# One adaLN transformer block: batch 1's projections made in two halves of tokens, the second half beside batch 1's own attention

## The chip, the core and the metric

The kernel runs on one core of a Trainium2 chip. The core has five engines that each work through their own list of instructions in order: PE (TensorE, matrix products), DVE (VectorE), ACT (ScalarE), POOL (GpSimd) and SP (SyncE, which here issues nearly all DMA transfers). They wait for one another through semaphores. The metric is the time of one execution on the device, in microseconds (us). All data are float32.

## The reference

Two batches of 1024 tokens, width 1024, go through one block. `c` gives six modulation vectors per batch (`sa, ca, ga, sb, cb, gb`). Then:

```
h   = layernorm(x) * (1 + ca) + sa
qkv = clip(h @ Wqkv.T, -8, 8);  q, k = layernorm(q), layernorm(k)   (over all 1024 columns)
p   = softmax(q k^T / sqrt(32) + slope_h * (key - query), causal)   32 heads of 32
x   = x + ga * ((p v) @ Wout.T)
h   = layernorm(x) * (1 + cb) + sb
x   = x + gb * ((silu(h Wg ag) * (h Wu au)) @ Wd ad)                2752 wide
```

The causal mask is what matters for the change: the first 512 queries of a batch need the keys and values of the first 512 tokens only.

## The kernel before, in words

**Dense products.** `seven` makes a 256-token by 1024-column product as seven block products of a Strassen-Winograd scheme (`SEVEN`), each of four matmuls of 128x128 by 128x512 on PE, into two alternating banks of PSUM. It takes seven weight tiles of 1 MB each (`B11 B21 T2 T1 T3 B22 T4`, made or loaded by `weights_b`). The pool of these tiles holds one set, so a tile of the next set can be loaded only when the last product that uses its predecessor is done. `read` takes each product out of PSUM on ACT or DVE. In this text "a product" is one of the seven.

**Projections.** `projections(b, ...)` (L927) makes Q, K and V of batch `b`: for each `part` (0, 1, 2) it gets the weights and then runs over the four pairs `j` of token tiles, 256 tokens each. The operand `a` of a pair is loaded from DRAM (1.8 MB). For Q and K the rows are normalized (`normalize`) and, during the following products, transposed on PE and taken to DRAM (`turned`, `todo`). V goes to DRAM directly. When V of an odd pair is out, `ready.add((b, j // 2))` says that this half of the batch's tokens can be attended to. `side` is called after every product and takes one step of `down_weights`, the preparation of weights for the last stage (POOL subtractions and small DMAs).

**Attention.** `attention` (L1013) is a generator over batches, blocks of 512 queries (`qb`) and groups of four heads (`k`, eight of them). A group consists of units (`jb`): four of them in the first query block, eight in the second, each a block of 128 keys. A unit is: scores on PE (four matmuls with 32 rows, in two halves), exponentials on ACT (L1069), the causal mask on POOL for diagonal blocks (L1073), and, two units later (`LAG`), the weighted sum of values on PE (`weigh`) and a running sum of the exponentials on DVE and POOL (L1101). After a group, `settle` sums over keys on PE in the one bank that transposes use too. The scores of a unit need the PSUM of the unit before, which its exponentials release. `chunk` loads a group's queries, keys and values, two groups ahead; it waits for `ready`.

**What sets the order.** `together(att, dense, share)` walks the attention generator and, after each step, takes dense work until its planned amount `d` reaches `share(a)`, a function of the planned attention `a` so far. `share` (L1569) gives `LEAD + DENSE0` units of dense work to batch 0's attention and `DENSE1` to batch 1's; these three constants stand at L1359. If `chunk` finds its tokens not ready it yields None, and `together` takes a dense step at once, share or not. The dense work is `dense_work` (L1535): the last V pairs of batch 0, all of batch 1's projections, then the output projection (`output`) of batch 0 and of the first half of batch 1. Within this stage PE's order is kept as emitted; the other engines' lists, SP's too, are ordered by the framework's scheduler. After the attention the rest of the output projection and the feed-forward layer follow.

Of the kernel before, what the change touches and what calls it, by code (L numbers as in the profile page):

```python
# [480 lines left out]
def kernel(  # L481
# [20 lines left out]
    B, S, D = x.shape  # L502
    INTER = wg_t.shape[1]
    KC = D // P
    NT = S // P
# [27 lines left out]
    wt_dram = [  # L533
        dram.tile([P, 4, KC // 2, HALF], FP, tag=f"wt_{r}", name=f"wt_{r}") for r in range(4)
    ]
# [253 lines left out]
    def weights_b(pool, w, nm, sums, other=None, swap=False):  # L789

        made = other is None
        order = ("B11", "B21", "T2", "T1", "T3", "B22", "T4") if made else ("B11", "B21", "B12", "B22", "T1", "T2", "T3", "T4")
        bt = {
            q: (other if q == "B12" or q == "B22" and swap else pool).tile(
                [P, KC // 2, HALF], FP, tag=f"w{q}", name=f"w{q}_{nm}"
            )
            for q in order
        }  # L800
        for q in order:
            if q in BLOCKS:
                kh, n = BLOCKS[q]
                nc.sync.dma_start(
                    bt[q], w[ds(kh * D // 2, D // 2), ds(n * HALF, HALF)].rearrange("(k p) f -> p k f", p=P)
                )
            elif made:
                nc.sync.dma_start(bt[q], sums[:, PARTS[q]])
        if not made:
            for k in range(KC // 2):  # L810
                nc.vector.tensor_sub(bt["T1"][:, k], bt["B12"][:, k], bt["B11"][:, k])
                nc.vector.tensor_sub(bt["T2"][:, k], bt["B22"][:, k], bt["T1"][:, k])
            for k in range(KC // 2):
                nc.gpsimd.tensor_sub(bt["T3"][:, k], bt["B22"][:, k], bt["B12"][:, k])
            for k in range(KC // 2):
                nc.gpsimd.tensor_sub(bt["T4"][:, k], bt["B21"][:, k], bt["T2"][:, k])
            for q in ("T1", "T2", "T3", "T4"):
                nc.sync.dma_start(sums[:, PARTS[q]], bt[q])
        return bt

    def seven(a, bt, banks, read, between, grain):

        x, y = banks.pair()
        for c_, qa, qb_, q in SEVEN:
            bank = x if c_ == "x" else y
            first = q in ("P1", "P2", "P5")
            for j in range(KC // 2):
                matmul(
                    bank, a(qa, j), bt[qb_][:, j, :],
                    start=(first and j == 0), stop=(j == KC // 2 - 1), skip_group_check=True,  # L830
                )
                if j % grain == grain - 1 and j < KC // 2 - 1:
                    banks.made += 1
                    yield grain * MM
                    yield from between(q)
            read(q, bank)
            banks.made += 1
            yield grain * MM
            yield from between(q)
# [17 lines left out]
    def column(t, r):  # L857
        return lambda k: t[:, r + k : r + k + 1]
# [43 lines left out]
    def tokens(b, j, todo, ap_, xp, sm):  # L902

        a = ap_.tile([P, 7, KC // 2, P], FP, tag="a", name=f"a_{b}_0_{j}")
        xs = []
        for m in range(2):
            xt = xp.tile([P, D], FP, tag="xt", name=f"xt_{b}_{j}_{m}", bufs=2)
            nc.scalar.dma_start(xt, x[b, ts(2 * j + m, P), :])
            xs.append(xt)
        normalize(xs, xs, sm, f"x{b}_{j}")()  # L910
        for m in range(2):
            for g in range(2):
                def go(bank, m=m, g=g):
                    q = (("A11", "A12"), ("S3", "A22"))[m][g]
                    turned(
                        xs[m], bank, lambda k: a[:, SLOT[q], k % 4, :],
                        lambda k: modt[:, 1, k, b : b + 1], lambda k: modt[:, 0, k, b : b + 1], g,
                    )
                    if (m, g) == (1, 1):
                        sums_a(a, nc.vector, nc.gpsimd)  # L920
                        nc.sync.dma_start(hop_dram[b][j], a)
                todo.add(go)
        return a
# [3 lines left out]
    def projections(b, pools, banks, places, extra=None, other=None, side=lambda n, e: None):  # L927

        ap_, wp_, rawp, partp, qsp, xp, sm = pools
        todo = Todo(banks)
        made = {}
        if b == 0:
            made[0] = tokens(b, 0, todo, ap_, xp, sm)
        for part in range(3):
            bt = weights_b(wp_, wqkv_t[:, ts(part, D)], f"{b}_{part}", wt_dram[part], other, b == 0 and part == 1)
            for j in range(NT // 2):
                if b == 0 and part == 2 and j == NT // 4:
                    yield "mark"  # L940
                if b == 0 and part == 0:
                    if j == 0:
                        yield from todo.run(len(todo.list), True)
                    a = made.pop(j)
                    if j + 1 < NT // 2:
                        made[j + 1] = tokens(b, j + 1, todo, ap_, xp, sm)
                else:
                    a = ap_.tile([P, 7, KC // 2, P], FP, tag="a", name=f"a_{b}_{part}_{j}")
                    nc.sync.dma_start(a, hop_dram[b][j])
                if extra is not None:  # L950
                    extra(todo, part * (NT // 2) + j)
                raws = [
                    rawp.tile([P, D], FP, tag="raw", name=f"raw_{b}_{part}_{j}_{m}") for m in range(2)
                ]
                part_t = {}
                q0, n = (2 - b, places) if b or part or j else (5, 4)

                def read(q, bank):
                    if q in ("P1", "U2", "P5"):
                        part_t[q] = partp.tile([P, 512], FP, tag=q, name=f"{q}_{b}_{part}_{j}")  # L960
                        nc.scalar.copy(part_t[q], bank)  # L961
                        return
                    m, n = QUAD[q]
                    dst = raws[m][:, ts(n, HALF)]
                    if q == "U6":
                        nc.vector.tensor_scalar(dst, bank, CLIP, -CLIP, ALU.min, ALU.max)
                    else:
                        nc.vector.tensor_add(dst, part_t[MATE[q]], bank)  # L968
                        nc.vector.tensor_scalar(dst, dst, CLIP, -CLIP, ALU.min, ALU.max)

                yield from seven(
                    lambda q, i: a[:, SLOT[q], i, :], bt, banks, read, 
                    todo.places(q0, n, lambda e: side(part * (NT // 2) + j, e)), KC // 2
                )
                yield from todo.run(len(todo.list), True)
                if part == 2:
                    for m in range(2):
                        nc.sync.dma_start(v_dram[b][:, 2 * j + m, :], raws[m])
                    if j % 2:
                        ready.add((b, j // 2))  # L980
                    continue
                todo.first(normalize(raws, raws, sm, f"qk{b}_{part}_{j}"), b == 0)
                qs = qsp.tile([P, KC, 2, P], FP, tag="qs", name=f"qs_{b}_{part}_{j}")
                r_w, r_b = ((R_QW, R_QB), (R_KW, R_KB))[part]
                for m in range(2):
                    for g in range(2):
                        def go(bank, m=m, g=g, raws=raws, qs=qs, r_w=r_w, r_b=r_b, part=part, j=j):
                            turned(
                                raws[m], bank, lambda k: qs[:, k, m, :], column(vt, r_w), column(vt, r_b), g, b == 0
                            )  # L990
                            if (m, g) == (1, 1):
                                nc.sync.dma_start(
                                    qk_dram[b][part][:, :, ds(2 * j * P, 2 * P)],
                                    qs.rearrange("p k m t -> p k (m t)"),
                                )
                        todo.add(go)
# [359 lines left out]


    OUT_US = 112.0
    LEAD, DENSE0, DENSE1 = 16.0, 370.0, 136.0  # L1359

    def halves(half, jb):
        return (nc.vector, nc.gpsimd)[half]
# [213 lines left out]
    opools, _, bt, todo, _ = out_args  # L1576
# [99 lines left out]
    with ExitStack() as ff:  # L1676
# [9 lines left out]
        with ExitStack() as gu:  # L1686
# [62 lines left out]
            count = [0]  # L1749
# [22 lines left out]
            for s in range(NSB):  # L1772
# [66 lines left out]
                for n_, (oa, ob, frm, to) in enumerate(STAGES):  # L1839
# [11 lines left out]
                    part = {"g": {}, "u": {}}  # L1851
# [6 lines left out]
                    for e, (c_, qa, qb_, q) in enumerate(CHAIN):  # L1858
                        bt = bts[e] if e < len(bts) else moving(s, n_, e)
# [231 lines left out]
```

## Time and profile before

| | |
|---|---|
| median of 3 runs | 2853.81 us (2849.35 to 2857.14) |
| the profiled execution, its own time | 2848.94 us |
| its span | 2846.9 us |
| PE, DVE, POOL, ACT busy over the span | 95%, 51%, 46%, 24% |
| granted TensorE clock, mean | 0.984 |
| DMA | 579.14 MB, mean 203 GB/s |

The span falls into three parts. Up to 362 us: modulation vectors and batch 0's projections. From 362 to about 1331 us: attention of both batches, with dense work between its steps. From there to the end: the rest of the output projection and the feed-forward layer, which are nearly all PE.

Within the middle part, the first matmul of scores of each block gives four stages. Batch 0's first query block runs from 362 to 538 us, its second to 937 us; batch 1's first query block to 1061 us, its second to the end of the attention.

A line of a group of instructions gives the line of the kernel, engine, operation, tiles, shapes and count, then busy time, the mean of one in ns, and the idle time of the engine before them with what ended it. A line of the timeline gives start and duration in us, the instruction, and in brackets the idle time before it. PE executes one float32 matmul of the program as two instructions, so "x8" is a product of four matmuls.

### The profile page before, as it was taken

How to read it: one execution, taken by the hardware profiler on the slowest of the kernel's cores; microseconds unless marked ns; L12 is line 12 of the kernel's file. 1: busy time of each engine (PE TensorE's matmuls, PEld its weight loads, DVE VectorE, ACT ScalarE, POOL GpSimd, SP SyncE). 2: the span in 40 equal slices, each digit the busy share in tenths (PEclk: the TensorE clock that was granted, in tenths of full speed). 3: DMA queues.
4: the chain of work that ended last, by engine and by line, in shares of the span. 5: the costliest groups of instructions: out<-in, count | busy, mean ns of one | idle time of the engine just before them, and what ended most of it. 6: DMA issues, size and time to landing. Idle time of an engine off the chain costs nothing. (4 is left out here: it accounts for less than half of the span.)

```text
span 2846.9 us, 29933 instructions
## 1 busy us (share of the span) xinstructions
PE 2691.8 (95%) x10271; PEld 1328.0 (47%) x10271; DVE 1462.4 (51%) x2285; ACT 687.8 (24%) x1524; POOL 1296.2 (46%) x1270
## 2 busy tenths in 40 slices
PE   6999999999999888889999999999999998999998
PEld 2444433333333222223664444444444447888776
DVE  5766525566634457666644453544536355443442
ACT  1322243444344556554111010110101101000000
POOL 3312124545565665655447474455636431322352
PEclk9999999999999899999999999999999999999999
DMA  9877863766755554433687576675857668554552
GB/s 346 310 273 300 298 233 118 234 217 209 231 152 198 149 175 136 147 128 112 199 294 244 170 251 214 186 279 162 278 176 234 199 198 267 150 148 136 167 144 79
DMA packets 377573, 579.14 MB, mean 203 GB/s; under 512 B 21590, under 2 KB 278712, under 8 KB 366276
## 3 DMA queue, kind: packets, MB, share of 16 engines
q1 hardware_dynamic: 363928, 556.12, 59.9%
q10 hardware_dynamic: 13484, 21.02, 2.3%
q8 instruction: 84, 1.38, 0.2%
q14 instruction: 77, 0.63, 0.1%
HBM read 411.89 MB, written 165.17 MB: 203 GB/s over the span
## 5 line engine op out<-in xcount | busy, mean ns | idle before, releaser
L1069 ACT ACTIVATE p<-sc,kw 128x128 f32<-128x128 f32 (+3 forms) x1024 | 422.5, 515 | 356.9 <-PE sc L743 344.4
L743 PE MATMUL bank<-wT,a 128*128 128x512 f32 x768 | 356.8, 608 | 15.1 <-ACT P L961 8.5
L1101 POOL TENSOR_TENSOR p<-p,p 128x1024 f32<-128x1024 f32 (+3 forms) x128 | 262.5, 2051 | 174.0 <-PE av L743 142.0
L1101 DVE TENSOR_TENSOR p<-p,p 128x1024 f32<-128x1024 f32 (+3 forms) x192 | 250.2, 1314 | 143.2 <-POOL p L1073 85.2
L743 PE MATMUL bank<-wB,a 128*128 128x512 f32 x576 | 262.3, 601 | 1.4 <-DVE raw L968 0.9
L743 PE MATMUL sc<-cq,ck 32*128 32x512 f32 (+3 forms) x1536 | 192.7, 540 | 55.9 <-ACT p L1069 55.6
L743 PEld LDWEIGHTS bank<-wT,a 128*128 128x128 f32 x768 | 141.2, 193 | 190.7 <-issue 163.2
L1073 POOL TENSOR_SCALAR_AFFINE_SELECT p<-p 128x256 f32<-128x256 f32 x256 | 136.7, 548 | 195.6 <-ACT p L1069 192.2
L743 PE MATMUL av<-p,cv 128*32 128x512 f32 (+3 forms) x1536 | 170.7, 512 | 3.2 <-POOL p L1073 3.2
L743 PEld LDWEIGHTS bank<-wB,a 128*128 128x128 f32 x576 | 104.6, 190 | 144.3 <-issue 126.1
L743 PEld LDWEIGHTS sc<-cq,ck 32*128 32x128 f32 x1536 | 64.6, 186 | 193.6 <-ACT p L1069 108.0
L1863 PE MATMUL gy<-bt,sig 128*128 128x512 f32 x280 | 132.2, 594 | 7.0 <-DVE gX L1670 6.9
L1863 PE MATMUL uy<-bt,siu 128*128 128x512 f32 x280 | 131.6, 592 | 0.0
L1863 PE MATMUL gx<-bt,sig 128*128 128x512 f32 x280 | 131.6, 592 | 0.0
L1863 PE MATMUL ux<-bt,siu 128*128 128x512 f32 x280 | 131.6, 592 | 0.0
L743 PEld LDWEIGHTS av<-p,cv 128*32 128x32 f32 x1536 | 33.7, 109 | 122.5 <-issue 83.5
L1863 PEld LDWEIGHTS gy<-bt,sig 128*128 128x128 f32 x280 | 52.7, 190 | 76.1 <-issue 64.1
L1863 PEld LDWEIGHTS ux<-bt,siu 128*128 128x128 f32 x280 | 53.2, 190 | 67.0 <-issue 66.5
L1863 PEld LDWEIGHTS uy<-bt,siu 128*128 128x128 f32 x280 | 53.2, 190 | 67.0 <-issue 65.3
L1863 PEld LDWEIGHTS gx<-bt,sig 128*128 128x128 f32 x280 | 53.2, 190 | 67.0 <-issue 65.7
L1863 PE MATMUL ux<-bt,wuS 128*128 128x512 f32 x160 | 75.2, 592 | 0.0
L1863 PE MATMUL gx<-bt,wgS 128*128 128x512 f32 x160 | 75.2, 592 | 0.0
(415 smaller groups left out, 4459.8 us busy)
## 6 DMA issues: line engine op xcount, KB each, us to landing
bt<-bop_T SPq DMA_DIRECT2D x140, 512.0 KB
bt<-bop_B SPq DMA_DIRECT2D x99, 512.0 KB
a<-hop SPq DMA_DIRECT2D x20, 1792.0 KB
wm<-in_L_wmod_dram SPq DMA_DIRECT2D x48, 512.0 KB
wB<-in_L_attn_Wqkv_dram SPq DMA_DIRECT2D x21, 1024.0 KB
aq_S<-act_S SPq DMA_DIRECT2D x16, 1280.0 KB
qk<-qs SPq DMA_DIRECT2D x16, 1024.0 KB
act_S<-asS SPq DMA_DIRECT2D x30, 512.0 KB
```

The costliest lines, as they stand in the source:

```text
L743: return in_order(nc.tensor.matmul(*args, **kw_))
L1069: last_exp[0] = nc.scalar.activation(p[:, g, lo:hi], sp[:, g, lo:hi], AF.Exp, bias=kw[:, d, h_ : h_ + 1])
L1073: last_mask[0] = nc.gpsimd.affine_select(out=p[:, :, 0:P], in_=p[:, :, 0:P], pattern=[[0, 2], [1, P]], compare_op=ALU.is_ge, fill=0.0, bas ...
L1101: adders[b](half, jb).tensor_add(dst, dst, ps[half][:, :, 0:n])
L1863: nc.tensor.matmul(ps.rearrange("p (j t) -> p j t", j=NJ), ins[mat][qa][:, c2, :], bt[:, :, c2, :], start=(q in ("P1", "P2", "P5") and c2 ...
```

## The change

For batch 0 nothing changes in `projections` but names. For batch 1 the loop over the three parts is run twice, first with the pairs 0 and 1 (tokens 0 to 511), then with the pairs 2 and 3: Q, K, V of the first half, then Q, K, V of the second. Each of the six runs gets its weights by `weights_b`, so that the three sets of seven tiles are loaded twice. The first half becomes `ready` when its V is out. `n_pair`, a count of pairs made, replaces the computed number in the call of `side`. `DENSE0` goes from 370 to 280, and `DENSE1` from 136 to 226.

```diff
-        for part in range(3):
-            bt = weights_b(wp_, wqkv_t[:, ts(part, D)], f"{b}_{part}", wt_dram[part], other, b == 0 and part == 1)
-            for j in range(NT // 2):
+
+        halves_ = [range(NT // 2)] if b == 0 else [range(NT // 4), range(NT // 4, NT // 2)]
+        count = itertools.count()
+        for js, part in itertools.product(halves_, range(3)):
+            bt = weights_b(
+                wp_, wqkv_t[:, ts(part, D)], f"{b}_{part}_{js[0]}", wt_dram[part], other, b == 0 and part == 1
+            )
+            for j in js:
+                n_pair = next(count)
...
-                    todo.places(q0, n, lambda e: side(part * (NT // 2) + j, e)), KC // 2
+                    todo.places(q0, n, lambda e: side(n_pair, e)), KC // 2
...
-    LEAD, DENSE0, DENSE1 = 16.0, 370.0, 136.0
+    LEAD, DENSE0, DENSE1 = 16.0, 280.0, 226.0
```

## The prediction

> **What bounds the kernel now.** I read the page first: busy shares, then the 40 slices.
>
> ```profile
> PE 2691.8 (95%) x10271; PEld 1328.0 (47%) x10271; DVE 1462.4 (51%) x2285; ACT 687.8 (24%) x1524; POOL 1296.2 (46%) x1270
> ...
> PE   6999999999999888889999999999999998999998
> PEclk9999999999999899999999999999999999999999
> ```
>
> PE is the bound over the whole; only slices 13 to 18, batch 1's attention, show eights. The busy time of the four stages (start:end, total, then PE, PEld, DVE, ACT, POOL busy, granted clock, DMA share, GB/s):
>
> ```profile
> 362.00:538.00 176.00, 171.44 (x837) 65.00 (x836) 77.82 (x129) 73.54 (x184) 73.02 (x100) 0.99 0.51 171
> 538.00:937.00 399.00, 382.12 (x1724) 139.77 (x1728) 218.48 (x307) 171.96 (x401) 221.74 (x197) 0.98 0.65 214
> 937.00:1061.00 124.00, 105.84 (x668) 35.08 (x660) 59.22 (x94) 67.96 (x173) 80.52 (x98) 0.89 0.51 150
> 1061.00:1328.00 267.00, 230.06 (x1325) 73.04 (x1324) 175.47 (x244) 159.32 (x375) 161.08 (x129) 0.97 0.40 124
> ```
>
> PE idles 21 us of 575 beside batch 0 and 55 us of 391 beside batch 1, where no other engine is full either. So batch 1 is bound by a chain. PE's waits from 362 to 1328 us name it (total, times, longest):
>
> ```profile
> PE sc L743 <- ACT p L1069: 55.6, 55, 3.8
> PE bank L746 <- DVE raw L727: 8.0, 3, 5.2
> PE bank L743 <- DVE h2t L849: 4.5, 1, 4.5
> PE bank L743 <- issue: 4.0, 1, 4.0
> ```
>
> Scores wait for the exponentials of the unit before, which hold their PSUM. The timeline shows both regimes. Batch 0, one unit with a whole product:
>
> ```profile
> 863.73 1.14 PE L743 MATMUL sc<-cq,ck 32*128 32x512 f32 x8
> 864.80 1.06 PE L743 MATMUL av<-p,cv 128*32 128x512 f32 x8
> 865.80 3.70 PE L743 MATMUL bank<-wB,a 128*128 128x512 f32 x8
> 869.43 1.14 PE L743 MATMUL sc<-cq,ck 32*128 32x512 f32 x8
> ```
>
> Batch 1, one unit with half a product, one with none:
>
> ```profile
> 1154.25 1.14 PE L743 MATMUL sc<-cq,ck 32*128 32x512 f32 x8
> 1155.32 1.06 PE L743 MATMUL bank<-p,ones 128*32 128x512 f32 x8
> 1156.20 1.04 PE L743 MATMUL av<-p,cv 128*32 128x512 f32 x8
> 1157.18 1.98 PE L743 MATMUL bank<-wT_o,aoS 128*128 128x512 f32 x4
> 1159.09 1.14 PE L743 MATMUL sc<-cq,ck 32*128 32x512 f32 x8
> 1160.16 1.07 PE L743 MATMUL av<-p,cv 128*32 128x512 f32 x8
> 1162.77 1.14 PE L743 MATMUL sc<-cq,ck 32*128 32x512 f32 x8 [1.55 <-ACT p L1069]
> ```
>
> From scores to scores a unit takes the longer of PE's own work and the exponentials' turn. The first unit takes 5.7 us (all PE), the last 3.7 us with 2.1 us of PE work.
>
> Lastly the handover to the output projection, whose weights overlay the projections' buffers:
>
> ```profile
> 899.04 1.14 PE L743 MATMUL sc<-cq,ck 32*128 32x512 f32 x8
> 900.12 1.06 PE L743 MATMUL bank<-p,ones 128*32 128x512 f32 x8
> 905.16 3.75 PE L743 MATMUL bank<-wB_o,aoA 128*128 128x512 f32 x4 [3.98 <-issue]
> ...
> 899.14 0.38 SPq L804 DMA_DIRECT2D wB_o<-in_L_attn_Wout_dram x1
> ```
>
> The load goes out when V's last product ends; its first matmul starts 6.0 us later. PE idles 3.98 us, and the half product then takes 3.75 us instead of 1.98.
>
> **What the Trainium skill says.** "TensorE: Matmul & The Clock Gate", section "What's actually happening": an idle window of about 3.4 us puts PE's clock to half until it has been busy as long. The trace agrees: 3.75 against 1.98 us above, and a granted clock of 0.89 in the stage with most idle time. "GPSIMD Engine Reference", section 1: POOL's SBUF interfaces are shared with DVE when DVE reads two SBUF inputs. POOL's 1024-wide additions average 2051 ns over all forms, the full ones 2850 ns beside batch 1. "DMA: Bandwidth & Descriptors", section "Anatomy of one DMA": engines do not wait on semaphores, the issuing sequencer does; so a weight load that waits for PE holds back whatever stands behind it on SP. The trace shows such waits, 28 us in all from 400 to 900 us on the weight lines L804 and L808, with no PE wait put down to a load except the handover.
>
> **The change, part by part.**
>
> *What it removes.* No matmul. PE's order of both programs, laid against the trace of before instruction by instruction, gives whole products per stage: 31, 67, 9.5, 24 before and 24, 50, 19.5, 37.5 after. So 24 products leave batch 0's stages. Half a product and one turn of four transposes more are left after the last scores: 0.5 x 3.63 + 0.6, about 2 us.
>
> *What moving them is worth.* For each of the 192 units I took PE's work (3.63 us a product; a full block's scores 1.06 and values 1.06, narrower ones 0.85, 0.64, 0.43; settling 1.06; four transposes 0.67) and the shortest time such a unit shows in the trace: full block 3.7, the 384, 256 and 128 wide ones 3.0, 2.4, 1.8, a group's first 2.5; longer for the first group, whose exponentials are cut in 16 (5.5, 5.0, 3.2, 1.8), and a little for the second (4.3, 3.7, 2.5). The longer of the two, summed:
>
> | stage | measured | by the rule before (PE work) | left over | by the rule after (PE work) |
> |---|---|---|---|---|
> | batch 0, first block | 175.9 | 176.5 (172.0) | -0.6 | 150.7 (143.9) |
> | batch 0, second | 398.6 | 388.2 (383.4) | 10.4 | 338.6 (319.0) |
> | batch 1, first | 124.5 | 112.1 (93.3) | 12.4 | 148.7 (132.3) |
> | batch 1, second (no last unit) | 266.5 | 246.7 (217.4) | 19.8 | 285.1 (269.1) |
> | sum | 965.5 | 923.5 (866.1) | 42.0 | 923.1 (864.3) |
>
> The gain is nil: batch 1's losses to exponentials fall from 48 to 32 us, but batch 0's rise from 9 to 27. Products of 3.63 us are lumpy: with five in eight units instead of seven, some units have none. Units whose PE work is over 0.3 us short of their exponentials number 5, 4, 13, 26 before and 8, 16, 12, 12 after: 48 both times.
>
> *What is left over.* Before: the handover 6.4; one turn of K that waits for its normalization (7.9, at 738 us); one settling that waits for the shared bank (6.8, at 1078 us); two smaller in the last stage (2.5, 3.7); the rest about 1.1 per group. After, by stage: 0, 2, 14, 24. The second stage loses its handover and is less crowded. The third gets the handover, and keeps about 5.5 of 12.4 since denser work keeps PE's clock up. The last has 37.5 products for 24, so its 13 us of waits on DVE become about 17, plus 7 as before. Sum 40.
>
> *The handover moved.* In the built order its four last products of V stand in one run (14.5 us, because keys and values of the second half are not ready), and the output's first matmul directly behind them. The 2.1 us that lay between before are gone: 6.0 us idle plus 2.5 us at half clock, 8.5. Both are in the 14. Behind it on SP stand seven weight tiles, the gate, two rows and then the values of the next group: 9.5 MB; at the 410 GB/s which the DMA slices show there, 24 us after V's end. The group needs them some 27 us after it. Cost 0; without that cover, up to 5.
>
> *21 MB more.* 21 tiles of 1 MB, 21 issues on SP. Batch 0's stages move 115 MB in 575 us; this brings the rate to about 260 GB/s, where slices reach 410. A tile becomes free seven products before its successor is needed, 50 us here. Loads of chunks stand behind them on SP: by the built order and the unit times above, the shortest gap (the handover apart) between PE freeing a buffer and needing its next content is 17.6 us after, 14.4 before. Cost 0, hidden under attention; a tile that came late costs at most the 6 us of the handover each. Below zero is excluded, since nothing is loaded earlier for it.
>
> *Weights preparation (`side`).* Same steps per product. About three sets of POOL work, 3 us each, move into batch 1's first block, where POOL is 65% busy: a mask later by at most 0.8 us, with two units of slack. Cost 0 to 3, taken 0.
>
> *Sum.* Rule -0.4, left over -2, tail +2: 0. The profiled execution's 2848.9 stays 2849; the median of runs lies 4.9 above it: 2854.
>
> **Rivals.** A measurement of this kernel can't tell less than about 0.3%, 8.5 us.
>
> *No change*, 2854, own range 2846 to 2862: the sum.
>
> *DVE becomes the chain beside batch 1's second block: slower.* Outside the running sums DVE does 97 us for 33.5 output products, 2.9 each; 13.5 more add 39 us: 214 of 305 us, 70% against 66%. For it: the settling at 1078 us waited for DVE's read of the one shared bank, behind two additions of 1.7 us. Against: 70% occurs before without stalls. Each such stall costs 6.8; from two more on it decides; four more give 2881.
>
> *The loads bind: slower.* Values at the handover 5 us late, two or three weight switches at 6: +20, 2874. Against: the gaps above.
>
> *Batch 0 pays only its PE work: faster.* If empty units next to full ones let exponentials run ahead, stages 1 and 2 lose not 27 but the 9 of before: -18, and with fewer half-clock stretches -22: 2832. Against: the scores' PSUM has no second buffer, and light units of batch 0 take 2.5 and 3.7 as in batch 1.
>
> That the change doesn't do what it says is excluded by the built order.
>
> **How the numbers follow.** No change 0.45, DVE 0.22, loads 0.13, faster 0.20. The edges of the first go over the bounds a little, to the slower side rather, as moved work meets new waits: faster 0.18, same 0.44, slower 0.38. The range leaves out a tenth on each side: from 2836 (most of the faster case) to 2882 (the DVE case).
>
> **What would show it.** Right: the first scores of batch 1 83 us earlier, near 853 us; batch 1's first block near 163 us and its second near 309; waits of scores on exponentials again near 55 us, about half of them before 853 us; a stall of 6 us before the first product with output weights. Wrong: a sum of those waits under 40 (the faster case), waits on DVE over 30 (the DVE case), or PE waits ended by loads.

## The result: 43 us slower, and the profile after

The changed kernel takes 2896.16 us (median of 4 runs, 2894.14 to 2898.79); the kernel before, run on the same chip, 2852.95 us. The ratio is 1.0151, 95% interval 1.0134 to 1.0169. The forecast was 2854, range 2836 to 2882: the time lies outside it.

The profiled execution of the changed kernel took 2895.27 us, with a span of 2893.4 us; before it was 2848.94. The page after, PE's busy share and the two rows of slices:

```profile
PE 2712.6 (94%) x10271; PEld 1338.1 (46%) x10271; DVE 1458.0 (50%) x2285; ACT 687.6 (24%) x1524; POOL 1291.5 (45%) x1270
...
PE   6999999989988979889989999999999998999998
PEclk9999999999998989999999999999999999999999
```

As many matmuls as before, and PE is busy 21 us longer: the same work ran at a lower clock. The eights and the seven of the attention now lie in slices 9 to 21, beside both batches; before they stood in slices 14 to 18 alone (not 13 to 18, as the prediction read them).

The four stages after, cut again at the first scores of each block (start:end, total, then PE, PEld, DVE, ACT, POOL busy, granted clock, DMA share, GB/s):

```profile
361.90:517.90 156.00, 148.76 (x763) 55.07 (x763) 61.12 (x93) 70.78 (x178) 64.49 (x88) 0.97 0.57 196
517.90:878.50 360.60, 323.14 (x1569) 116.22 (x1568) 195.90 (x267) 167.82 (x394) 207.46 (x187) 0.96 0.64 212
878.50:1043.60 165.10, 143.34 (x766) 53.79 (x767) 66.75 (x112) 70.94 (x178) 70.62 (x97) 0.91 0.56 184
1043.60:1367.00 323.40, 288.09 (x1444) 95.40 (x1444) 199.27 (x296) 162.64 (x382) 185.71 (x149) 0.93 0.53 160
```

The totals make 1005.1 us against 965.6 before: 39.5 of the 46.3 us between the two profiled executions. Batch 0 became shorter by 58 us, batch 1 longer by 97. The granted clock fell in three stages (0.99, 0.98 and 0.97 before, 0.97, 0.96 and 0.93 now). The rest, 7 us, comes after the scores of the attention's last unit.

PE's waits between 362 and 1367 us in the changed kernel (total, times, longest):

```profile
PE sc L743 <- ACT p L1075: 59.1, 57, 3.9
PE bank L746 <- DVE raw L727: 15.0, 3, 7.7
PE bank L746 <- DVE h2t L849: 10.3, 4, 4.5
PE bank L743 <- DMA wB_o<-in_L_attn_Wout_dram: 6.3, 1, 6.3
```

The waits on exponentials hardly rose (55.6 before). The waits on DVE, with two smaller lines not shown (qs 3.9, xr 3.4), make 32.6 us against 13.4 before. All of them are transposes (L746) that wait for DVE to finish what they transpose, or to read the bank that they share.

The longest of them, in the timeline:

```profile
600.75 9.91 POOL L1107 TENSOR_TENSOR p<-p,p 128x1024 f32<-128x1024 f32 x3 [14.57 <-PE av L743]
601.98 6.48 DVE L1107 TENSOR_TENSOR p<-p,p 128x1024 f32<-128x1024 f32 x2
...
608.38 2.29 DVE L722 TENSOR_TENSOR fix_qk<-rstd_qk 128x2 f32<-128x2 f32 x1
...
611.65 2.30 DVE L724 TENSOR_SCALAR fix_qk<-fix_qk 128x2 f32<-128x2 f32 x1
...
615.06 1.11 PE L746 MATMUL bank<-ident,raw 128*128 128x128 f32 x4 [7.75 <-DVE raw L727]
```

While POOL adds running sums (L1107), DVE's own two sums take 3.24 us each, and two steps on 128x2 values take 2.3 us, where such steps take 0.16 to 0.17 us with POOL idle. The normalization of K is late, the transposes that stand next in PE's order wait for it, and scores and values stand behind them. Afterwards the transposes take 1.11 us instead of 0.66, and the eight matmuls that follow them 5.61 us instead of 3.70: PE's clock has been halved.

The trace before had this already. The turn at 738 us that the prediction counted as a wait for normalization met a sum on POOL in the same way:

```profile
737.35 3.19 POOL L1101 TENSOR_TENSOR p<-p,p 128x1024 f32<-128x1024 f32 x1
738.27 2.29 DVE L722 TENSOR_TENSOR fix_qk<-rstd_qk 128x2 f32<-128x2 f32 x1
...
743.75 1.12 PE L746 MATMUL bank<-ident,raw 128*128 128x128 f32 x4 [5.16 <-DVE raw L727]
```

In the attention, 128x2 steps of over 1 us number six before and eight after, each beside a sum on POOL.

The clock also falls after much shorter gaps. PE alone, batch 0's first block:

```profile
404.25 0.64 PE L743 MATMUL av<-p,cv 128*32 128x256 f32 x8
405.68 0.91 PE L743 MATMUL sc<-cq,ck 32*128 32x384 f32 x4 [0.79 <-ACT p L1075]
406.83 0.92 PE L743 MATMUL sc<-cq,ck 32*128 32x384 f32 x4 [0.24 <-ACT p L1075]
407.68 5.40 PE L743 MATMUL bank<-wT,a 128*128 128x512 f32 x8
```

This is a unit without dense work. Two gaps of 1.03 us together, and the next product takes 5.40 us instead of 3.70. The same two gaps stand at six places of this kernel; at five the clock was halved after them, at one not:

```profile
977.39 0.91 PE L743 MATMUL sc<-cq,ck 32*128 32x384 f32 x4 [0.78 <-ACT p L1075]
978.54 0.91 PE L743 MATMUL sc<-cq,ck 32*128 32x384 f32 x4 [0.24 <-ACT p L1075]
979.39 0.66 PE L746 MATMUL bank<-ident,raw 128*128 128x128 f32 x4
979.88 3.60 PE L743 MATMUL bank<-wB,a 128*128 128x512 f32 x8
```

The trace also records the granted clock itself. In the four stages it is halved 19 times; in the 3.4 us before, PE was idle for 0.9 to 3.4 us, and only twice for all of it.

Where PE's attention time went, over the four stages. "Half clock" is the duration of PE's instructions in the stretches whose recorded clock is half, less the median of the same instructions at full clock. "Over its price" is what remains of PE's busy time beyond the half clock and the prices of the prediction's rule:

| us | before | after | difference |
|---|---|---|---|
| waits on exponentials | 55.0 | 59.7 | +4.7 |
| waits on DVE | 13.4 | 32.6 | +19.2 |
| handover's and values' loads | 4.0 | 7.9 | +3.9 |
| waits on POOL's masks | 3.2 | 1.8 | -1.4 |
| half clock | 23.6 | 42.2 | +18.6 |
| PE's work over its price | -0.6 | -3.2 | -2.6 |
| PE's work at the rule's prices | 866.1 | 864.3 | -1.8 |
| sum | | | +40.6 (measured +39.4) |

### The profile page after: what moved, and what is told of

Read it like the earlier page. It is cut to its first block, busy times and chain, and to the rows that moved or that the text cites. A ratio compares the mean times of both kernels' runs of the same rounds, so it can differ in the third digit from the quotient of the medians.

```text
span 2893.4 us, 29968 instructions
## 1 busy us (share of the span) xinstructions
PE 2712.6 (94%) x10271; PEld 1338.1 (46%) x10271; DVE 1458.0 (50%) x2285; ACT 687.6 (24%) x1524; POOL 1291.5 (45%) x1270
## 5 line engine op out<-in xcount | busy, mean ns | idle before, releaser
L743 PE MATMUL bank<-wT,a 128*128 128x512 f32 x768 | 365.6, 620 | 14.1 <-ACT P L967 7.5
L1107 POOL TENSOR_TENSOR p<-p,p 128x1024 f32<-128x1024 f32 (+3 forms) x128 | 265.5, 2074 | 176.9 <-PE av L743 133.7
L1107 DVE TENSOR_TENSOR p<-p,p 128x1024 f32<-128x1024 f32 (+3 forms) x192 | 241.8, 1271 | 120.5 <-POOL p L1079 70.3
L743 PE MATMUL bank<-wB,a 128*128 128x512 f32 x576 | 268.1, 611 | 1.3 <-DVE raw L974 0.7
L743 PE MATMUL sc<-cq,ck 32*128 32x512 f32 (+3 forms) x1536 | 196.8, 554 | 59.3 <-ACT p L1075 59.1
L1079 POOL TENSOR_SCALAR_AFFINE_SELECT p<-p 128x256 f32<-128x256 f32 x256 | 126.1, 504 | 225.5 <-ACT p L1075 207.7
L849 DVE TENSOR_SCALAR qs<-bank,vt 128x128 f32<-128x128 f32 x144 | 50.1, 403 | 57.3 <-PE bank L746 56.6
```

The source lines that it names most:

```text
L743: return in_order(nc.tensor.matmul(*args, **kw_))
L849: nc.vector.tensor_scalar(dst(k), tp[:, j, :], mul(k), add(k), ALU.mult, ALU.add)
L1079: last_mask[0] = nc.gpsimd.affine_select(out=p[:, :, 0:P], in_=p[:, :, 0:P], pattern=[[0, 2], [1, P]], compare_op=ALU.is_ge, fill=0.0, bas ...
L1107: adders[b](half, jb).tensor_add(dst, dst, ps[half][:, :, 0:n])
```

## The experiments

Two theories stood at first. *Turns:* PE's transposes come too early for a DVE that POOL slows. *Lumps:* whole products thinned out beside batch 0 leave units with too little PE work, and gaps cost clock. Against them stood the rival of the loads: the weights read twice, 21 MB more. "Turn" below means four transposes and DVE's copy out of the bank; a ratio is to the kernel before, run beside it.

### The halves with the old pace

```diff
-    LEAD, DENSE0, DENSE1 = 16.0, 280.0, 226.0
+    LEAD, DENSE0, DENSE1 = 16.0, 370.0, 136.0
```

> The changed loop (two halves, weights loaded twice, 21 MB more) with the constants of before (370, 136). PE's order is then that of before but for which part a product belongs to: products per stage are the same, and the rule gives 927.5 us against 923.5 before. DVE theory (the loss comes from PE's transposes waiting for DVE, because dense work was moved beside batch 1): within 10 us of before, ratio 1.000 to 1.004. Load theory (the loss comes from loading the weights twice and from the loads at part switches): at least 15 us slower than before, ratio above 1.005, with PE waits ended by DMA or by weights.

Measured: 2858.96 us, ratio 1.0018 (1.0008 to 1.0029). The new order of the parts and the doubled weight loads cost about 5 us together (2 to 8). The other 38 us come with the moved share of dense work. The loads' theory falls: in the changed kernel, too, PE's waits on loads are only 7.9 us.

### Half products for batch 1

```diff
-                    todo.places(q0, n, lambda e: side(n_pair, e)), KC // 2
+                    todo.places(q0, n, lambda e: side(n_pair, e)), KC // 2 if b == 0 else 2
```

The dense stream of batch 1's projections can then be cut after two matmuls of a product's four. Turns are handed out and `side` is called at each cut, so both come faster: the last step of the weights' preparation on POOL starts at 689 us, not 946. No run separates that from the smaller pieces.

> The changed kernel with batch 1's projections handed out by half products (two matmuls, as the output projection has them), not whole ones. Units short of work fall from 48 to 23 by the built order, and the rule's sum from 923.1 to 893.8 us. If the rule holds and lumps of whole products are what kept the gain at nil: 20 to 35 us faster than the changed kernel (2862 to 2877). If waits on DVE take over what is filled in: within 8 us of the changed kernel (2888 to 2904).

Measured: 2858.51 us, ratio 1.0021 (1.0012 to 1.003), 38 us less than the changed kernel and a little more than expected. PE's waits on exponentials from 362 to 1375 us, where they were 59.1:

```profile
PE sc L743 <- ACT p L1075: 27.4, 24, 3.8
```

Batch 0's two stages fall from 516.6 to 485.5 us. The waits on DVE nearly stay (28.6 us in the attention, for 32.6), and the half clock keeps 29.2 us of 42.2. So the lumps are real, and they are not the same thing as the waits on DVE. Nor are they most of the miss: the waits that went are those that the rule had priced, and of what it had not priced only the 13 us of half clock and 4 us of waits on DVE came back.

### Turns later, in three kernels

In the changed kernel (first run) and in the kernel before (second), turns of batch 1's Q and K start two products later, and those of the output's rows two later as well:

```diff
-                q0, n = (2 - b, places) if b or part or j else (5, 4)
+                q0, n = (2 + b, places) if b or part or j else (5, 4)
...
-    def output(b, js, pools, banks, bt, todo, keep, q0=1):
+    def output(b, js, pools, banks, bt, todo, keep, q0=3):
```

> The changed kernel, with the transposes of batch 1's pairs and of the output pairs placed two products later within the next pair (from the fourth product on, not the second), so that normalization on DVE has more time before PE reaches them. The rule gives 922.7 us, the changed kernel 923.1. DVE theory: PE's waits for DVE fall from 32.6 us to under 12, half-clock time with them, and the kernel is 20 to 35 us faster than the changed one (2862 to 2877). Load theory: within 8 us of the changed kernel (2888 to 2904).

> The kernel before with the same later transposes. Its waits for DVE were 13.4 us with about 8 us of half clock behind them; DVE theory: 5 to 20 us faster than before (ratio 0.993 to 0.998). Load theory says nothing of it: if later transposes cost as much as they save, within 4 us of before.

Measured: 2880.92 us, ratio 1.0089 (1.0063 to 1.0115), for the changed kernel; 2882.73 us, ratio 1.0108 (1.0083 to 1.0132), for the kernel before, which became 31 us slower where I expected it faster. The first gained 15 us, less than the 20 to 35 expected. PE's waits of the changed kernel with late turns:

```profile
PE sc L743 <- ACT p L1075: 59.3, 55, 3.9
PE bank L746 <- DVE qs L849: 17.2, 7, 6.3
```

The waits on the normalization (15.0) are gone. In their place turns wait for DVE's copy of the turn before (qs): started later, they bunch at the end of a pair, where the code hands out all that are left, and all go through one bank. So, as I read it, a turn has a window: too early it waits for its rows, too late for the bank.

The third kernel moves the output's turns only, where no bunching was seen:

> The changed kernel, with later transposes for the output pairs alone; batch 1's projections keep theirs. In the run with both, batch 1's second block took 309.7 us for 323.4, and the stages of the projections 679 for 682. If the two are separate: 310 us in that stage, the first three as in the changed kernel within 4 us, 2878 to 2884 in all. If the later transposes of the projections did the gain: no gain here.

Measured: 2883.93 us, ratio 1.0113 (1.0075 to 1.015), from two runs. The last stage falls from 323.4 to 309.6 us and the other three stay within 0.3. So early turns cost that stage 13.8 us. All three kernels pay for the output's late turns after the attention, where PE then waits 11.5 to 11.9 us for the load of `hl`, an operand of the work behind; neither kernel does so with early turns.

### Batch 0's running sums on DVE alone

```diff
+    def vector_only(half, jb):
+        return nc.vector
...
-    together(attention(apools, (halves, mostly), banks), dense_work(), share)
+    together(attention(apools, (vector_only, mostly), banks), dense_work(), share)
```

This gives DVE more work and takes POOL off the buffers that both use. If DVE were short of time, it would get slower; if sharing stretches its instructions, faster.

> The changed kernel, with batch 0's running sums of exponentials all on DVE; POOL keeps the masks and the weights. DVE gets some 8 us more per group of the second block. Sharing theory (DVE is late because its instructions take 2 to 3 us while POOL adds beside it): the wide sums on DVE take about 1.2 us each in batch 0, the two- and three-microsecond small steps of normalization vanish, waits on DVE in batch 0's second block fall from 15 us to under 6, and the kernel is 5 to 20 us faster. Load theory of DVE (it has too much to do): those waits grow, the kernel is 5 to 30 us slower.

Measured: 2879.26 us, ratio 1.0091 (1.0067 to 1.0115), 17 us less than the changed kernel. DVE's groups by shape in batch 0's second block, from 518 to 878 us (count, busy time, mean ns, idle time before). The changed kernel:

```profile
L1107 DVE TENSOR_TENSOR p<-p,p 128x1024 f32<-128x1024 f32 x32 | 68.3, 2133 | 15.1 <-POOL p L1079 5.5 <-PE av L743 5.2 <-ACT p L1075 3.0
...
L722 DVE TENSOR_TENSOR fix_qk<-rstd_qk 128x2 f32<-128x2 f32 x6 | 7.9, 1317 | 11.9 <-ACT rstd_qk L720 11.9
```

The same groups' first line with batch 0's sums on DVE:

```profile
L1107 DVE TENSOR_TENSOR p<-p,p 128x1024 f32<-128x1024 f32 x64 | 75.6, 1227 | 15.7 <-POOL p L1079 6.5 <-PE av L743 5.5 <-ACT p L1075 3.7
```

Twice as many wide sums cost DVE 7.3 us more. The other 32 on POOL had bought next to nothing. L722, a step on 128x2 values, falls from 1317 ns to 154, and PE's waits on the normalization (raw) from 15.0 to 5.7 us.

### All running sums on DVE, in both kernels

```diff
-    together(attention(apools, (halves, mostly), banks), dense_work(), share)
+    together(attention(apools, (vector_only, vector_only), banks), dense_work(), share)
```

> The kernel before, with the running sums of both batches all on DVE; POOL keeps masks, weights and the output's work. PE's order and the rule's sum (923.5) stay. Sharing theory (DVE's instructions are slow while POOL adds beside it, so that PE's transposes wait): the waits on DVE, 13.4 us, fall under 6, half-clock time with them; 5 to 15 us faster than before. If DVE has too much to do with all sums: 5 us or more slower.

> The changed kernel with the sums of both batches on DVE. With batch 0's alone it took 2879 us, and batch 1's second block kept its 323 us, 38 over the rule. Sharing theory: that block falls to 300 to 310 us, waits on DVE from 32.6 us to under 15, and the kernel to 2858 to 2870. If the output's normalization itself is what PE waits for there: that block stays above 318 us, the kernel near 2879.

Measured: the kernel before with this edit 2834.04 us, ratio 0.9943 (0.9921 to 0.9964); the changed kernel with it 2866.07 us, ratio 1.0048 (1.0034 to 1.0063). The edit gains 0.57% in the one and 1.03% in the other. So sums on POOL cost the kernel before some 16 us too, and the changed kernel 30. No step on 128x2 values takes over 1 us in either. The waits on DVE fall less than expected, in the attention from 13.4 to 9.3 us and from 32.6 to 18.0.

### Half products with other shares

With half products and the later turns of the output, the share of dense work beside batch 0 is raised again, to 310 and to 340, and once to 300 with all sums on DVE (where `DENSE1` is 196, not the 186 that the expectation names):

```diff
-    LEAD, DENSE0, DENSE1 = 16.0, 280.0, 226.0
+    LEAD, DENSE0, DENSE1 = 16.0, 310.0, 196.0
```

> Half products, later output transposes and the constants 310 and 196 together: the handover then has attention between V's last product and the output's first. The rule gives 892.6 us. Left over like the half-product run in batch 0 (18), half of its 17 in batch 1's first block, and 26 or less in the second: 930 to 945 for the four stages against 965.6 before; 2815 to 2835 in all, below the kernel before. If waits move on again: 2850.

> The same with the constants 340 and 166. The rule gives 903.0 us, 10 more than with 310, with fewer output products beside the sums of batch 1 (less waiting on DVE there). If DVE's waits are what is left: within 5 us of the run with 310; if the rule decides: 8 to 12 us slower.

> Half products, later output transposes, all sums on DVE, and the constants 300 and 186, which leave some 9 us more dense work after the attention to cover the loads of the rest stage (a wait of 12.0 us in the run with 310). The rule gives 884.6 us, before 923.5. If what is left over falls to 40: the four stages take 925 for 965.6, and with 9 us more behind them the kernel takes 2815 to 2832. If waits move on once more: 2840 to 2856.

Measured: 2856.02 us, ratio 1.0025 (1.0016 to 1.0035), at 310; 2878.02, ratio 1.01 (1.0073 to 1.0126), at 340; 2843.67, ratio 0.9979 (0.9969 to 0.9988), at 300 with the sums on DVE. The first and the last missed their ranges; the step from 310 to 340 was 22 us, about twice what the rule of the prediction gives. Other waits come up. At 310 one comes after the attention:

```profile
1352.88 0.60 PE L746 MATMUL bank<-ident,xr 128*128 128x128 f32 x4
1365.49 6.51 PE L743 MATMUL rest<-hl,restw 128*128 128x256 f32 x16 [12.01 <-DMA hl<-h]
```

These are 12.01 us of idle PE before the load of `hl` is there. It is the wait of the output's late turns, not of the share: at 340 it is 12.2 us, and at 300, whose shares leave 10 us more dense work behind the attention, it is gone. At 340 one turn also waits 11.8 us for the bank, at 300 one product 7.4 us for DVE's read of its bank. The rule prices units; it does not see these.

### Both edits, in both kernels

Half products for batch 1 and all sums on DVE: in the changed kernel with its own shares (280 and 226), and in the kernel before with its own.

> The changed kernel with its own constants (280, 226), half products in batch 1's projections and all sums on DVE. Half products alone took 38 us off the changed kernel, the sums alone 30. If the two causes (lumps of whole products that leave units short and the clock at half; DVE slow beside POOL) are separate: the savings add, 2825 to 2835, batch 0's two stages at 475 to 480 us and batch 1's at 458 to 470. If they are one cause seen twice: no more than 8 us under half products alone, 2850 to 2858.

> The kernel before with the same two edits. The rule's sum falls from 923.5 to 916.2, since batch 0 had few units short of work. If the rule decides: 3 to 9 us faster than with the sums alone (2834), so 2825 to 2831. If more pieces mean more collisions with DVE: not faster than 2834.

Measured: the changed kernel 2830.4 us, ratio 0.9935 (0.9917 to 0.9953), inside the expected 2825 to 2835 and faster than both kernels of this study. The two gains add up: 1.30% and 1.03% from 1.0151 would give 0.9918. Its half clock takes 17.7 us, less than the 23.6 before, its waits on exponentials 26.5. But the kernel before with the sums on DVE alone, at 0.9943, lies within that interval: no run shows that the two halves themselves are worth anything.

The kernel before with both edits takes 2863.03 us, ratio 1.0052 (1.0034 to 1.007), 29 us more than with the sums alone and far from what I expected. Most of that is one stall of PE. SP's queue and PE in that run, and below them the same pair of tokens in the kernel before with the sums alone:

```profile
572.05 0.32 SPq L1121 DMA_DIRECT2D rc<-sum  x1
...
576.55 0.32 SPq L1125 DMA_DIRECT2D rec<-rc  x1
576.96 0.39 SPq L804 DMA_DIRECT2D wB<-in_L_attn_Wqkv_dram  x1
577.44 0.46 SPq L808 DMA_DIRECT2D wT<-wt  x1
577.95 0.42 SPq L949 DMA_DIRECT2D a<-hop  x1
...
589.20 3.75 PE L743 MATMUL bank<-wB,a 128*128 128x512 f32 x4 [19.99 <-issue]
```

```profile
530.50 0.42 SPq L949 DMA_DIRECT2D a<-hop  x1
...
568.39 3.70 PE L743 MATMUL bank<-wB,a 128*128 128x512 f32 x8
```

PE stands from 569.2 to 589.2 us before the first product of a pair. It needs the tile `B11`, whose load went out at 551.26, and the pair's operand `a`. The load of `a` went out at 577.95, behind the block's reciprocals of the softmax sums on SP, which had waited 5.9 us and then 3.6 us for their own data, and behind two weight tiles. By the trace's record of transfers it landed at 589.1; the `wB` issued ahead of it, at 576.96, is another tile and landed at 582.2. In the kernel with the sums alone the same load went out at 530.50. That the stall is this load is read from these times; no run moved the load alone, and why it stands so late on SP is not shown. So this run doesn't tell what half products are worth to the kernel before; it shows what an operand's load late in SP's queue can cost.

## Why the prediction was wrong

**The rule for units: right.** It gave 923.5 us before and 923.1 after. Measured waits on exponentials beside batch 0 rose from 9.4 to 25.2 us (predicted: 9 to 27), and beside batch 1 fell from 45.6 to 34.5 (48 to 32). For the units the nil gain is what happened.

**What is left over: wrong, and this step carries the miss.** It was 42 us before and was put at 40; it measured 82. By stage, with the terms of the table above (the last column also holds idle PE time not put down to anything):

| stage | predicted | measured | waits on DVE | half clock | PE's work over its price | loads, masks | exponentials beyond the rule, rest |
|---|---|---|---|---|---|---|---|
| batch 0, first | 0 | 5.3 | 0 | 5.0 | -0.1 | 0 | 0.4 |
| batch 0, second | 2 | 22.0 | 18.9 | 11.5 | -7.3 | 0 | -1.1 |
| batch 1, first | 14 | 16.4 | 0 | 11.2 | -0.2 | 6.3 | -0.9 |
| batch 1, second | 24 | 38.3 | 13.7 | 14.5 | 4.4 | 3.4 | 2.3 |

Two terms of it were mis-sized.

- "The second stage loses its handover and is less crowded": 2 us. The waits on DVE there were 8.0 and became 18.9, though DVE was no busier (54% of the stage against 55%). The half clock there was 5.3 us and became 11.5. I judged DVE by its busy share. What decides is how long one normalization takes when it meets POOL's sums, and whether PE's order has the transposes directly behind it. The runs with the sums on DVE show the stretching to be a cause. Why these meetings cost more in the changed kernel than before is not settled: the sums are the same, the stretched steps eight for six, and where they meet a normalization is an accident of the order.
- In the last stage I scaled the waits on DVE by the number of products, 13 to 17, and these measured 13.7, but I allowed 7 for all else. The half clock alone took 14.5, where it had taken 6.1. I had expected denser work to keep the clock up; in batch 1's first stage, where I said so, it took 11.2 us for 10.5.

**The clock.** The prediction priced the half clock only after long gaps, as the Trainium skill describes it ("TensorE: Matmul & The Clock Gate", section "What's actually happening": an idle window of about 3.4 us). The trace shows it after gaps of 0.79 and 0.24 us between scores and values, though not each time. The measurement decides: what has to be priced is a stretch of light work with gaps, not one long gap. The trace before shows it too: its clock record is halved at 1005.7 us behind the same two gaps. I also named 0.89 the clock of "the stage with most idle time"; the last stage idled longer (37 us for 18) at 0.97. Gaps beside batch 0 that the rule counted at their bare length cost clock as well; with both kinds of gaps reduced (half products and sums on DVE) the half clock takes 17.7 us.

**DVE and POOL.** The same skill ("GPSIMD Engine Reference", section 1, Specifications) says that they share SBUF interfaces, with contention among others when DVE reads two SBUF inputs. The prediction quoted that and put POOL's slow additions beside it, but gave DVE's side no price. The traces give it: 2133 ns with POOL's sums beside and 1227 ns without. The step L724, which reads a single tensor, was stretched as well, to 2.30 us.

**The handover: right.** Predicted 8.5 us with the half clock; its wait was 6.27, and the product after it took 3.75 us. The values behind it: 0, at most 5; measured 1.6.

**21 MB more: right.** Cost 0; the halves with the old pace lose about 5 us in all, the order of the parts included.

**Tail: too small.** Predicted +2, measured +7.1 from the last unit's scores to the end. A turn there waits 3.07 us on DVE, but before one waited 3.1 us too; the half clock took 7.5 us of the tail for 3.7. The rest is open.

**The sum.** Rule -0.4, left over +40, tail +7.1: +46.7, against +46.3 between the profiled executions.

**The signs named.** The first scores of batch 1 came at 878.5 us, not 853. Batch 1's first block took 165.1 (163 predicted), its second 323.4 (309). The waits on exponentials were 59.1 (55), the stall at the handover 6.3 (6). "Waits on DVE over 30" was the sign of the DVE rival, and 32.6 came.

**The rivals.** The DVE rival named the right engine and, with 2881 us, came nearest, but placed the waits in batch 1's second block only and grounded them in DVE's busy time. DVE was busy for 62% of that block, not 70%; over half of the waits lie beside batch 0, and the half clock was not in its price. The loads' rival is out. The faster rival said that batch 0 loses only 9 us of its units, which would give 2832. Scores did not run ahead, as argued against it. Half products remove most of that loss by another means; that they and the sums on DVE together give 2830.4 is no sign that this rival was right.

## What to carry to other kernels

When dense work is spread thinner between latency-bound steps, cut it into smaller pieces too: with whole 3.6 us products some steps get none, and PE has gaps and then loses its clock. A busy share of 55% doesn't say that an engine is on time: look at the longest duration of its small instructions and at who stands behind them in PE's order. Work handed to POOL to relieve DVE has to be weighed against what it does to DVE's own instructions.

## What the runs showed of the hardware

- PE ran at half speed after idle gaps of 0.79 and 0.24 us in a stretch of scores and values: a product of 5.40 us instead of 3.70. The same gaps did so at five of six places of the changed kernel. Of 19 falls of the clock in its attention, only two followed 3.4 us without any work on PE.
- Additions of 128x1024 on DVE average 2133 ns while POOL does such additions too, up to 3.24 us each, and 1227 ns without. A step on 128x2 values took 2.3 us beside one of POOL's additions instead of 0.16 to 0.17. Taking 32 such additions from POOL cost DVE 7.3 us in all.
- On SP an operand's load that was issued after a block's reciprocals stood behind 9.5 us of waits, and PE stood 20 us.
